# A graph-attention layer: the last 64 edges in one column, the last sums loaded early, the closing projections reordered behind 16 unused products, and the few rows handled later

## The chip, the cores and the metric

The kernel runs on one core of a Trainium2 chip. The core has five engines with a queue each: PE (TensorE, matrix products), DVE (VectorE), ACT (ScalarE), POOL (GpSimd) and SP (SyncE, here only for issuing DMAs). The metric is the device time of one execution in microseconds (us), as the median of repeated runs. Less is better.

## The reference

N = 12500 nodes, E = 212500 edges sorted by destination, 128 features, 8 heads of 16, float32. Cut to what matters:

```python
h = relu(layernorm(x))
q, k, v = h @ Wq.T + bq, edge_attr @ Wk.T + bk, h @ Wv.T + bv
qs, qd = q[src], q[dst]
in_m, out_m, diag_m = sum(qs * k), sum(qd * k), sum(qs * qd)     # per head
score = (softmax(in_m / 4) + softmax(out_m / 4) + softmax(diag_m / 4)) * edge_weight
                                  # softmax over the edges of one destination
h = segment_sum(score * v[dst], dst)
out = x + leaky_relu(h @ Wo.T + bo, 0.1)
```

Since v[dst] is the same for all edges of a destination, a node's h is v times a sum over its edges of exp terms with and without the edge's weight; only these sums (2 x 24 numbers a node) are gathered over edges.

## The kernel before, in words

The edges are cut into 415 groups of 512 (four columns of 128), in five segments of 83 blocks; group g is block t = g // 5 of segment s = g % 5. The last 84 edges don't fill a group. Of these, 64 form a block 83 (called G in the code) that is done after the loop, and the last 20 are the "few rows", done apart.

For each group the loop does: `turn` (PE transposes the 512 edge rows, L1273, and ACT copies them, L1275), `project` (PE: k, L1281 and its bias L1282), `spread_q` (PE: a one-hot times a window of q's rows gives qd, L1289, copied by ACT, L1292), `logits` (DVE: three products, L1300 to L1302, and a reduction, L1303). The rows q[src] come by an indirect DMA that GpSimd issues (L719), four to a group, 26 groups ahead (`LOOK`), into a ring of 28 tiles; the gather for group g + 26 waits on purpose for the projection of group g. SP loads windows (L690), edges (L699), edge bounds (`heads` L742, `tops` L745) and sources (L642). In groups 0 to 4 ACT also issues five DMAs that blank the DRAM tables `sums[s]` (L1778). Every five groups, a block's segment maxima are scanned (DVE), exponentials taken (ACT, L1413), and the sums over each destination's edges made as products with one-hot selections (PE, L1459, and L1470 for the last three blocks) and written to `sums[s]` (`put_rows`, L1480).

The order of every engine's queue is fixed by the order in which the code is written (`pin`). So an instruction that waits holds back all that stand behind it on its engine.

The few rows: `gather_few` (L757 to L763) loads their 20 edge rows and gathers 40 rows of q by one indirect DMA on POOL (L760), which stands behind 116 other gathers; `part_few` (L766) copies 20 of these rows within the chip by a DMA on SP, in group 1; `logits_few` (L1338 to L1358) makes their logits in group 6, in small steps on PE, ACT and DVE.

The nodes: most (two units of 256 nodes at a time) are finished inside the loop. For the rest, the end after the loop does: blocks G-2 = 81, G-1 = 82 and G = 83 (`powers`, `weigh_powers`, `show_ends`, `to_rows`, `put_rows`), then the two pairs of units called `leaving` and `last_pair`, then five groups of the object list `rest` (r0 to r4; r4 is half a group). A group's steps are: `load_last` (L1182: the sums, of two segments for some nodes: `ends_ab` and `more`), a join of the two (L1823), `halves_of` (L1146), `scores_of` (DVE, L1150 to L1153), `weigh` (L1224: v times score), `turn` (PE transposes, L1203, ACT copy to hT, L1206), `project_o` (PE: bias L1209 and product L1211; ACT: scaled copy, L1235), `add_x` (maximum L1241, addition of x L1242) and `store` (L1248, L1250). Before the change, SP loads `ends_ab` and ACT loads `more`, both after the puts; DVE joins r0 and GpSimd r1 to r4; each group is turned and projected before the next one is turned.

Of the kernel before, what the change touches and what calls it, by code (L numbers as in the profile page):

```python
# [16 lines left out]
HEADS = 8  # L17
# [455 lines left out]
def ordered_path(ctx: ExitStack, tc: tile.TileContext, flag, x, src, dst, edge_attr, edge_weight,  # L473
# [184 lines left out]
    def fetch(t):  # L658
# [16 lines left out]
        to = [mybir.EngineType.SP] if t < G else [mybir.EngineType.SP, mybir.EngineType.Activation]  # L675
# [3 lines left out]
        if t == G:  # L679
            for inst in loads:  # L680
                pin(inst)
# [473 lines left out]
    class Nodes:  # L1155
# [51 lines left out]

        def product(self, to, bias, w):
            pin(nc.tensor.matmul(to[:, :self.n, :], ones3, bias[:, :self.n, :], start=True, stop=False))  # L1209
            for b in range(self.n):  # L1210
                pin(nc.tensor.matmul(to[:, b, :], self.hT[:, b, :], w, start=False,  # L1211
                                     stop=(b == self.n - 1)))
# [17 lines left out]
        def project_o(self, to):  # L1230
            n = self.n
            self.product(to, bo3, wo)
            o = self.h[:, :n]
            self.held = to
            pin(nc.scalar.activation(o, to[:, :n], AF.Copy, scale=SLOPE))  # L1235
# [8 lines left out]
        def store(self):  # L1244
            for i, u in enumerate(self.of):
                y = self.x[:, 2 * i:2 * i + 2, :].rearrange("p k f -> p (k f)")
                if u < NU - 1:
                    pin(nc.sync.dma_start(units(out, u, 1, F)[:, 0, :], y))  # L1248
                else:
                    pin(nc.sync.dma_start(out[u * UN:, :].rearrange("(p k) f -> p (k f)", k=2),  # L1250
                                          y[:LAST, :]))
# [13 lines left out]
    with tc.tile_pool(name="work", bufs=2) as work, \  # L1265
# [19 lines left out]
        def spread_q(g):  # L1285
# [7 lines left out]
            del ohs[g]  # L1293
# [16 lines left out]
        for i in range(2):  # L1310
            ends_t.append(scan.tile([K4, P], BF, name=f"ends_t{i + 2}", bufs=1))
            nc.vector.memset(ends_t[-1][0:1, :], 1.0)

# [73 lines left out]
        def scan_back(t):  # L1387
# [5 lines left out]
            else:  # L1393
                head = st[t - 1]["head"]
                m = d["m"] = scan.tile([R, HEAD], F32, name="m_end", bufs=1)
                pin(nc.vector.tensor_sub(m, head, l_end))

        def turn_max(t):
            d = st[t]
            n, width = (P, BE) if t < G else (HEAD // JN, HEAD)  # L1400
            m_ps = d["mT"] = small([P, JN, R], "m_ps")
            for j in range(JN):
                pin(nc.tensor.transpose(m_ps[:n, j, :], d["m"][:, j:width:JN], ident[:R, :R]))  # L1403

        def powers(t):
            d = st[t]
            mT = d["mT"].rearrange("p j (s c) -> p j s c", s=S)
            if t < G:
                back = work.tile([P, JN, S, 2, H3], F32, name="back")
# [4 lines left out]
                d["weigh"] = [(back, 0, JN)]  # L1414
                del lTs[t]
            else:
                n = HEAD // JN
                d["back"], d["weigh"] = [], []
                for j in range(0, JN, 2):
                    half = fin.tile([P, JN, F], F32, name="x_in", bufs=5).rearrange("p j f -> p (j f)")  # L1420
                    half = half[:, :2 * S * 2 * H3].rearrange("p (j s i c) -> p j s i c", j=2, s=S, i=2)
                    pin(nc.scalar.activation(half[:n, :, :, 0, :], mT[:n, j:j + 2], AF.Exp, scale=-SCALE))
                    d["back"] += [half[:, 0], half[:, 1]]
                    d["weigh"].append((half, j, j + 2))

        def weigh_powers(t):
            at, part = block_rows(t)
            n = P if t < G else HEAD // JN
            for back, lo, hi in st[t]["weigh"]:
                att = att_t[:, part, lo:hi].rearrange("p (s b) j -> p j s b", b=G)[:, :, :, at:at + 1]  # L1430
                pin(nc.vector.tensor_mul(back[:n, :, :, 1, :], back[:n, :, :, 0, :],  # L1431
                                         att[:n].to_broadcast([n, hi - lo, S, H3])))

        def select(t):
            at, part = block_rows(t)
            ends = ends_t[t % 2 if t < G - 1 else t - G + 3]
            pin(nc.sync.dma_start(ends[1:, :], rel_d[part].rearrange("(s b) (j p) -> s b j p", b=G, j=JN)
                                  [:, at, :, :]))

        def show_ends(t):  # L1440

            sel = st[t]["sel"] = work.tile([P, JN, S, W], F32, name="sel", bufs=3)
            for i in range(0, JN, 2):
                d = small([P, 2, S, W], "d_ps")
                pin(nc.tensor.matmul(d.rearrange("p j s w -> p (j s w)"), ends_t[t % 2 if t < G - 1 else t - G + 3],
# [5 lines left out]
        def to_rows(t):  # L1451
            d = st[t]
            n = P if t < G else HEAD // JN
# [14 lines left out]
            for s in range(S):  # L1468
                for j in range(JN):
                    pin(nc.tensor.matmul(w_ps[:, s, :], d["sel"][:n, j, s, :],  # L1470
                                         d["back"][j][:n, s].rearrange("p i c -> p (i c)"),
                                         start=(s == 0 and j == 0), stop=(s == S - 1 and j == JN - 1)))
            pin(nc.scalar.copy(rows[:W, :S], w_ps))
# [61 lines left out]
        def begin_rest(at):  # L1535
# [14 lines left out]
            if at == DRAIN - 1:  # L1550
                for of in rest:
                    of.more = None
                    if any(len(parts_of(u)) > 1 for u in of.of):
# [3 lines left out]
                        pin(nc.gpsimd.memset(of.more, 0.0))  # L1557
# [91 lines left out]
        def show():  # L1649
            pin(nc.vector.tensor_copy(shows, show_end.rearrange("k (s j) -> k j s", j=JN)[:, :, :, None]  # L1650
                                      .to_broadcast([K4, JN, S, W])))
            pin(nc.vector.tensor_copy(shows[0:1], show_row[:, None, None, :].to_broadcast([1, JN, S, W])))

# [47 lines left out]
        for g in range(end):  # L1701
# [67 lines left out]
            if 0 < g <= S + 1:  # L1769
                load_bounds(g - 1)  # L1770
            if g == 7:
# [16 lines left out]
        turn_max(G - 2)  # L1788
        scan_on(G)
# [12 lines left out]
        weigh_powers(G - 1)  # L1802
        to_rows(G - 1)
        put_rows(G - 1)
# [79 lines left out]
```

## Time and profile before

| | us |
|---|---|
| median of 3 runs (lowest, highest) | 2182.34 (2178.96, 2182.61) |
| the profiled execution | 2183.8 |
| its span | 2182.0 |
| busy: PE, DVE, ACT, POOL | 1705.6, 1991.4, 1384.9, 1594.6 |
| end of the loop's last reduction (L1303) | 2123.6 |
| last store issued (L1250) | 2175.5 |
| mean granted PE clock | 0.831 |

How to read what follows: a group row of the page has line, engine, operation, tiles, count, then busy us and the mean ns of one, then the idle time before it and what ended it. A row of the waits has who waited, for whom, then us in total, times, and the longest. A row of a timeline has the start, the length, the engine, the line and the operation; in brackets the engine's idle time before it and what ended it. `x8` means that so many instructions stand in that row, and "issue" that nothing the profile shows was waited for. ACTq, SPq and POOLq are the engines' DMA issues. A row of the windows has the stretch, its length, the busy time and count of PE, PEld (weight loads), DVE, ACT and POOL, the granted PE clock, the DMA engines' mean busy share and GB/s.

### The profile page before, as it was taken

Reading aid. Unit: us, or ns where it says so; the run is one execution under the profiler, and the core shown is the slowest. Engines: PE = TensorE matmul, PEld = TensorE weight load, DVE = VectorE, ACT = ScalarE, POOL = GpSimd, SP = SyncE. Lnnn points to the kernel's source line nnn. Section 1 sums busy time; section 2 is a strip of 40 time slices with the busy share of each in tenths; the row PEclk is TensorE's granted clock in tenths of the full one; section 3 lists DMA queues with packets and bytes.
Section 4 is the critical chain, followed back from the end, with each engine's and each line's share of the span. In section 5 each row is a group of like instructions: output and inputs, shape, how many; then the busy total and the mean of one; then the engine's idle time right before and its main releaser. Section 6 shows DMA issues by size and latency. Waiting matters only on the chain.

```text
span 2182.0 us, 36286 instructions
## 1 busy us (share of the span) xinstructions
PE 1705.6 (78%) x10956; PEld 1327.6 (61%) x10956; DVE 1991.4 (91%) x2785; ACT 1384.9 (63%) x2743; POOL 1594.6 (73%) x1683
## 2 busy tenths in 40 slices
PE   5757878887878888888888888877777777678885
PEld 3546756665666666666666666655565565556664
DVE  6758899999999999999999999999898899898995
ACT  5656866666666666666666666665555665566672
POOL 7775677777777777777777777777777777777761
PEclk8877888898888988888878888887888898888786
DMA  9756466666667667665665755566555655556632
GB/s 258 216 159 187 136 174 169 174 166 183 167 173 180 176 170 190 171 168 155 168 172 147 184 158 163 147 163 158 159 143 146 160 156 163 148 154 164 164 92 65
DMA packets 370345, 356.97 MB, mean 164 GB/s; under 512 B 189022, under 2 KB 285097, under 8 KB 369933
## 3 DMA queue, kind: packets, MB, share of 16 engines
q1 hardware_dynamic: 301403, 239.37, 40.1%
q0 software_dynamic: 53152, 108.92, 19.8%
q10 hardware_dynamic: 15584, 6.27, 1.1%
q8 instruction: 89, 1.46, 0.3%
q14 instruction: 117, 0.96, 0.1%
HBM read 322.10 MB, written 32.22 MB: 162 GB/s over the span
## 4 chain that ended last, share of the span: by engine, by line
DVE 42%; DMA 20%; issue 12%; PE 12%; POOL 7%; ACT 5%; SPq 2%; DVEq 0%; ACTq 0%; POOLq 0%
DMA qq<-q_table,sources 16%; DVE lT L1303 11%; POOL qq L719 7%; DVE prod L1300 6%; DVE prod L1301 6%; DVE prod L1302 6%; PE k_ps L1281 3%; DVE l_ps L1363 3%; DVE m L1391 2%; DVE back L1412 2%; PE eT_ps L1273 1%; PE w_ps L1459 1%; DMA ea<-in_edge_attr_dram 1%; DVE back L1431 1%; PE node_ps L1211 1%
## 5 line engine op out<-in xcount | busy, mean ns | idle before, releaser
L719 POOL DMA_INDIRECT qq<-q_table,sources x1564 | 1487.0, 951 | 501.8 <-issue 328.6
L1303 DVE TENSOR_REDUCE lT<-prod 128x96 f32<-128x1536 f32 x415 | 727.4, 1753 | 14.3
L1281 PE MATMUL k_ps<-wk,eT 128*128 128x128 f32 x3320 | 563.5, 324 | 95.3 <-DVE prod L1302 89.9
L1281 PEld LDWEIGHTS k_ps<-wk,eT 128*128 128x128 f32 x3320 | 502.8, 232 | 139.6 <-DVE prod L1302 133.5
L1273 PE MATMUL eT_ps<-ident,ea 128*128 128x128 f32 x1660 | 305.6, 314 | 199.7 <-ACT eT L1275 129.3
L1273 PEld LDWEIGHTS eT_ps<-ident,ea 128*128 128x128 f32 x1660 | 223.2, 162 | 244.8 <-ACT eT L1275 160.9
L1300 DVE TENSOR_TENSOR prod<-qq,k_ps 128x512 f32<-128x512 f32 x412 | 279.1, 678 | 65.4 <-DMA qq<-q_table,sources 51.5
L1301 DVE TENSOR_TENSOR prod<-qq,qd_ps 128x512 f32<-128x512 f32 x412 | 279.9, 679 | 30.7 <-ACT qd L1292 30.6
L710 ACT ACTIVATE relb<-relb,before 126x512 bf16<-126x512 bf16 x415 | 302.4, 729 | 0.0
L1275 ACT COPY eT<-eT_ps 128x512 f32<-128x512 f32 x415 | 241.6, 582 | 66.9 <-PE eT_ps L1273 39.5
L1302 DVE TENSOR_TENSOR prod<-qd,k_ps 128x512 f32<-128x512 f32 x415 | 281.7, 679 | 0.0
L1292 ACT COPY qd<-qd_ps 128x512 f32<-128x512 f32 x415 | 236.8, 570 | 66.1 <-PE qd_ps L1289 65.7
L711 ACT ACTIVATE oh<-relb 126x512 bf16<-126x512 bf16 x415 | 261.4, 630 | 13.2
L1413 ACT ACTIVATE back<-back 128x480 f32<-128x480 f32 x83 | 50.1, 603 | 287.4 <-DVE back L1412 284.0
L1459 PE MATMUL w_ps<-back,sel 128*126 128x144 f32 (+1 forms) x1296 | 169.0, 288 | 41.9 <-ACT sel L1449 40.3
L1459 PEld LDWEIGHTS w_ps<-back,sel 128*126 128x126 f32 (+1 forms) x1296 | 156.7, 186 | 50.2 <-ACT sel L1449 48.6
L1289 PE MATMUL qd_ps<-win,oh 126*128 126x128 bf16 x1660 | 182.7, 239 | 0.0
L1282 PE MATMUL k_ps<-b,ones 3*128 3x512 bf16 x415 | 181.3, 437 | 0.0
L1289 PEld LDWEIGHTS <-oh 126*128 126x128 bf16 x1660 | 103.9, 104 | 115.0 <-issue 115.0
L1366 ACT COPY carry<-l_ps 120x1 f32<-120x1 f32 x81 | 12.9, 159 | 226.5 <-DVE l_ps L1363 221.1
L1403 PE MATMUL m_ps<-ident,m 120*128 120x120 f32 x332 | 75.5, 366 | 42.3 <-DVE m L1391 41.9
L1391 DVE TENSOR_TENSOR_SCAN m<-far,head,l_ps 120x512 f32<-120x512 bf16 x81 | 102.9, 1271 | 0.0
(237 smaller groups left out, 1835.4 us busy)
## 6 DMA issues: line engine op xcount, KB each, us to landing
ea<-in_edge_attr_dram SPq DMA_DIRECT2D x83, 768.0 KB
relb<-rel_d SPq DMA_DIRECT2D x83, 630.0 KB
ea<-in_edge_attr_dram SPq DMA_DIRECT2D x83, 512.0 KB
qq<-q_table,sources POOLq DMA_INDIRECT x1564
win<-q_table SPq DMA_DIRECT2D x415, 31.5 KB
far<-far_d SPq DMA_DIRECT2D x42, 270.0 KB
q_table<-q SPq DMA_DIRECT2D x24, 384.0 KB
sums<-rows SPq DMA_DIRECT2D x411, 7.9 KB
```

Of the source, the lines that this page charges most:

```text
L710: pin(nc.scalar.activation(d, d, AF.Abs, bias=before[:K3]))
L711: pin(nc.scalar.activation(oh, d, AF.Relu, bias=1.0, scale=-1.0))
L719: rows = pin(nc.gpsimd.indirect_dma_start(out=qq[:, j, :], out_offset=None, in_=x if g < RAW else q_table, in_offset=bass.IndirectOffsetOn ...
L1273: pin(nc.tensor.transpose(eT_ps[:, j, :], eas[g][:, j * F:(j + 1) * F], ident))
L1275: pin(nc.scalar.copy(eT, eT_ps))
L1281: pin(nc.tensor.matmul(k_ps[:, j, :], eTs[g][:, j, :], wk, start=(j == 0), stop=False))
L1289: pin(nc.tensor.matmul(qd_ps[:, j, :], ohs[g][:, j * P:(j + 1) * P], d["win"][:, s, :], start=(j == 0), stop=(j == JN - 1)))
L1300: pin(nc.vector.tensor_mul(prod[:, :, 0, :], qqs[g], ks[g]))
L1301: pin(nc.vector.tensor_mul(prod[:, :, 1, :], qqs[g], q_ps[g]))
L1302: pin(nc.vector.tensor_mul(prod[:, :, 2, :], qds[g], ks[g]))
L1303: pin(nc.vector.tensor_reduce(lTs[t][:, :, s, :], prod.rearrange("p j i (h d) -> p j (i h) d", d=DIM), AX.X, ALU.add))
L1459: pin(nc.tensor.matmul(w_ps[:(hi - lo) * W, lo:hi].rearrange("p s c -> p (s c)"), d["sel"][:n, j, lo:hi, :].rearrange("p s w -> p (s w)"), ...
```

## The change

1. **The few rows later.** `part_few` is issued in group 16 (block 3) instead of group 1, `logits_few` in group 21 (block 4) instead of group 6. The gather on POOL stays where it is.
2. **The last 64 edges in one column.** Block G used four columns of 16 edges; now it has 64 partitions and one column: 1 transposition for 4, 5 products for 20, one exponential and one weighing for two. Its weights are loaded by four small DMAs (`load_att`) in groups 54, 59, 64 and 69, its selection uses a table `shows_g` made in group 7.
3. **The order of the end.** Block G's steps now come before those of block G-1; the row copy of G-1 is on DVE; two of its five puts go to ACT's queue; `leaving` is projected after the last pair's turn.
4. **The sums.** The second parts (`more`) are loaded in group 409 by SP, and no longer cleared by GpSimd; their halves are added early; the first parts are loaded by SP. DVE joins r0 and r1, GpSimd r2 to r4, and only the columns that have two parts.
5. **Turnings a group ahead.** The five biases of `rest` are issued early (`begin_product`), each group is turned before the product of the group ahead of it, and 16 products into a PSUM tile that nothing reads (`unused`) stand between the biases and r0's turn.
6. **Stores.** The four of `leaving` and `last_pair` and the very last one are issued by ACT.

```diff
-                if t == 0:
+                if t == 3:
                     part_few(rows_few)
-                elif t == 1:
+                elif t == 4:
                     logits_few()
...
+            if s == 4 and 10 <= t < 10 + JN:
+                load_att(t - 10)
...
+        def begin_product(self, to, bias):
+            pin(nc.tensor.matmul(to[:, :self.n, :], ones3, bias[:, :self.n, :], start=True, stop=False))
...
-            if at == DRAIN - 1:
+            if at == 6:
...
-                        pin(nc.gpsimd.memset(of.more, 0.0))
+                        of.load_last(of.more, nc.sync, 1)
...
         scan_back(G - 1)
         powers(G - 2)
+        scan_back(G)
         turn_max(G - 1)
-        scan_back(G)
-        show_ends(G)
         turn_max(G)
-        leaving.project_o(small([P, JN, F], "node_ps"))
+        weigh_powers(G - 2)
+        to_rows(G - 2)
+        powers(G)
         powers(G - 1)
-        weigh_powers(G - 2)
-        powers(G)
-        to_rows(G - 2)
         put_rows(G - 2)
-        weigh_powers(G - 1)
-        to_rows(G - 1)
-        put_rows(G - 1)
         weigh_powers(G)
-        leaving.add_x(nc.vector)
-        leaving.store()
         to_rows(G)
         put_rows(G, q=nc.scalar)
-        for which, q in ((0, nc.sync), (1, nc.scalar)):
-            for r, of in enumerate(rest):
-                of.load_last(ends_ab[:, r * JN:r * JN + of.n] if which == 0 else of.more, q, which)
+        weigh_powers(G - 1)
+        to_rows(G - 1, nc.vector.tensor_copy)
+        put_rows(G - 1, range(3))
+        put_rows(G - 1, range(3, S), nc.scalar)
+        for of in rest:
+            if of.more is not None:
+                halves_of(of.more[:, of.both], nc.gpsimd)
         last_pair.scores()
         last_pair.weigh(last_pair.held)
         last_pair.turn(small([P, JN, P], "node_ps"))
+        leaving.project_o(small([P, JN, F], "node_ps"))
         last_pair.project_o(small([P, JN, F], "node_ps"))
+        leaving.add_x(nc.vector)
+        leaving.store(nc.scalar)
         last_pair.add_x(nc.vector)
-        last_pair.store()
+        last_pair.store(nc.scalar)
...
+        for r, of in enumerate(rest):
+            of.load_last(ends_ab[:, r * JN:r * JN + of.n], nc.sync, 0)
+            of.begin_product(places_o[r], bo3)
+        unused = small([P, JN, F], "unused")
+        for _ in range(16):
+            pin(nc.tensor.matmul(unused.rearrange("p j f -> p (j f)"), minus_b[:K3, :], now["oh"],
+                                 start=True, stop=True))
...
+        for r in range(2, len(rest)):
+            join(r, nc.gpsimd)
+        begin_end(0)
+        for r in range(1, len(rest) - 1):
+            begin_end(r)
+            rest[r - 1].project_o(places_o[r - 1], begun=True)
+            if r > 1:
+                leave(r - 2)
+        rest[-2].project_o(places_o[-2], begun=True)
+        begin_end(len(rest) - 1)
+        leave(len(rest) - 3)
+        rest[-1].project_o(places_o[-1], begun=True)
+        leave(len(rest) - 2)
+        leave(len(rest) - 1, nc.scalar)
```

`begin_end(r)` is the join (for r0 and r1), the scores, the weighing and the turn of group r; `leave(r)` is its `add_x` (GpSimd's addition for r0 to r2, DVE's for r3 and r4) and its store.

**Where it moves instructions.** SP's queue about group 1, before. `qq<-qq` is the copy of part_few, `win` a window of q's rows, `heads` and `tops` the edge bounds:

```order
L642 DMA sources<-in_src_dram 128x5x4
L766 DMA qq<-qq 20x128
L690 ISA
L690 DMA win<-q_table 126x128
L742 DMA heads<-in_dst_dram 1x84x1
L745 DMA tops<-in_dst_dram 1x84x1
L666 DMA relb<-rel_d 126x5x512
```

And the same place after the change:

```order
L642 DMA sources<-in_src_dram 128x5x4
L690 ISA
L690 DMA win<-q_table 126x128
L742 DMA heads<-in_dst_dram 1x84x1
L745 DMA tops<-in_dst_dram 1x84x1
L666 DMA relb<-rel_d 126x5x512
```

The copy no longer stands between the sources and the window; the same rows follow each other without it, and it comes three loads of sources later.

PE's queue after the loop, before. `node_ps<-ident,h` is the turn of the last pair, `node_ps<-ident,qq` that of a group of `rest`, `ones` with `b` a bias, and `wo` a projection:

```order
L1211 MATMUL node_ps<-wo,hT 128x128 x4
L1470 MATMUL w_ps<-back,sel 42x48 x40
L1470 MATMUL w_ps<-x_in,sel 42x48 x20
L1203 MATMUL node_ps<-ident,h 128x128 x4
L1209 LDWEIGHTS ones_90
L1209 MATMUL node_ps<-b_96,ones_90 128x512
L1211 MATMUL node_ps<-wo,hT 128x128 x4
L1203 MATMUL node_ps<-ident,qq 128x128 x4
L1209 LDWEIGHTS ones_90
L1209 MATMUL eT_ps<-b_96,ones_90 128x512
L1211 MATMUL eT_ps<-wo,qq 128x128 x4
L1203 MATMUL node_ps<-ident,qq 128x128 x4
```

After, the row products of blocks G-2, G and G-1 and the projections behind them:

```order
L1495 MATMUL w_ps<-back,sel 42x48 x20
L1495 MATMUL w_ps<-x_in,sel 42x48 x5
L1495 MATMUL w_ps<-back,sel 42x48 x20
L1203 MATMUL node_ps<-ident,h 128x128 x4
L1209 LDWEIGHTS ones_90
L1209 MATMUL node_ps<-b_96,ones_90 128x512
L1215 MATMUL node_ps<-wo,hT 128x128 x4
```

The products of the 64 edges stand between those of the two whole blocks and are 5 in place of 20, and `leaving`'s projection, which stood ahead of them all, has come behind the last pair's turn. Behind the last pair's projection stand the five biases, 16 products like the first row below, and then:

```order
L1859 MATMUL unused<-oh,minus_b 128x512
L1203 MATMUL node_ps<-ident,qq 128x128 x8
L1215 MATMUL eT_ps<-wo,qq 128x128 x4
L1203 MATMUL node_ps<-ident,qq 128x128 x4
L1215 MATMUL k_ps<-wo,qq 128x128 x4
L1203 MATMUL node_ps<-ident,qq 128x128 x4
L1215 MATMUL qd_ps<-wo,qq 128x128 x4
L1215 MATMUL k_ps<-wo,qq 128x128 x4
```

Two turns stand ahead of the first projection, and each later turn but the last one stands a group ahead of its projection.

More of the change, by code (lines that the diff above doesn't have):

```diff
@@ L1292, in spread_q @@
             pin(nc.scalar.copy(qds[g], qd_ps))
-            del ohs[g]
+            now["oh"] = ohs.pop(g)
         def logits(g):
@@ L1426, in weigh_powers @@
-        def weigh_powers(t):
-            at, part = block_rows(t)
[L1428 to L1432, printed above, removed]
+                back = fin.tile([P, JN, F], F32, name="x_in", bufs=5).rearrange("p j f -> p (j f)")
```

133 lines of the change are left out of this document (82 added, 51 removed).

## The prediction

> **What bounds the kernel now.** I read the page first (its spans, groups and slices), then GpSimd's waits and its gathers after 272 us, then the waits of the first 165 us, then the end after the loop. The profiled execution took 2183.8 us, a span of 2182.0 and 1.8 around it, 1.5 above the median of the three runs (2182.34); sums are made against the span, and the last step goes back to the median.
>
> From the page, the costliest group; then GpSimd's gathers from 272 us on, and its waits between 120 and 330 us:
>
> ```profile
> L719 POOL DMA_INDIRECT qq<-q_table,sources x1564 | 1487.0, 951 | 501.8 <-issue 328.6
> L719 POOL DMA_INDIRECT qq<-q_table,sources x1468: 940/945/1421, 272.4 to 2115.5; - x184
> POOL qq L719 <- issue: 32.3, 106, 0.3
> POOL qq L719 <- PE k_ps L1282: 26.3, 12, 6.4
> POOL qq L719 <- DMA tops<-in_dst_dram: 2.1, 1, 2.1
> ```
>
> From 272.4 to 2115.5 us GpSimd issues 1468 gathers, one every (2115.5 - 272.4) / 1467 = 1.256 us: 0.945 of work and the 0.30 that every gather has before it as "issue". That is a stream without a hole, over 85% of the span. VectorE is busier (91% on the page), but it needs the gathered rows, so the stream sets when the loop ends. Whatever lets it stand earlier at 272 us lets the loop end earlier by as much. Before that it has holes: 13 waits of 28.4 us together, less 13 x 0.30 of ordinary issue, 24.5 us. Twelve of them are for the projection of the group 26 before (L1282), whose place in the ring the gather takes. So that stage is paced by the groups, not by GpSimd. Why the groups are late stands in SyncE's and the other waits of the first stage:
>
> ```profile
> SPq L766 <- DMA qq<-q_table,few_i: 16.4, 1, 16.4
> PE eT_ps L1273 <- ACT eT L1275: 19.5, 1, 19.5
> ACT eT L1275 <- DMA tops<-in_dst_dram: 19.2, 1, 19.2
> 138.16 1.65 ACT L733 ACTIVATE qq<-qq,raw_shift,raw_inv 128x128 f32<-128x128 f32 x4
> 158.60 0.38 ACTq L1778 DMA_DIRECT2D sums<-jp  x1
> 154.07 0.85 SPq L766 DMA_DIRECT2D qq<-qq  x1
> 155.14 0.37 SPq L690 DMA_DIRECT2D win<-q_table  x1
> 156.43 0.76 SPq L745 DMA_DIRECT2D tops<-in_dst_dram  x1
> 151.77 0.92 POOL L760 DMA_INDIRECT qq<-q_table,few_i  x1 [0.30 <-issue]
> ```
>
> SyncE stands 16.4 us at the copy of part_few (L766), which it issues at 154.07. That copy needs the gather of the few rows, which stands in GpSimd's queue at 151.77. Behind the copy on SyncE stand the window load, heads and tops (156.43). ScalarE's third blanking store (L1778) needs the tops load; ScalarE is done with its work at 138.16 + 1.65 = 139.81 and issues at 158.60. TensorE, whose transposes wait for a copy behind that store, stands for 19.5 us.
>
> **The change part by part.** *Few rows later.* part_few moves from group 1 to group 16, logits_few from group 6 to group 21. The few gather stays at 151.77, so the copy at group 16 finds it landed and waits for nothing. SyncE's next instruction, the window load, now waits only for what else L766 waited for: the 16.4 us row is the part of its wait that came last, so SyncE goes on at 154.07 - 16.4 = 137.67. The copy's own slot goes as well (155.14 - 154.07 = 1.07). Tops is issued at 156.43 - 17.47 = 138.96, and the blanking store at 158.60 - 17.47 = 141.13, 1.3 after ScalarE is free. So the groups behind it start 17.5 us earlier, if nothing else is late next. What may be late next is the DMA:
>
> ```profile
> 100.00:140.00 40.00, 32.28 (x225) 25.75 (x224) 27.38 (x58) 32.23 (x73) 30.24 (x33) 0.91 0.80 226
> 140.00:160.00 20.00, 0.53 (x3) 0.34 (x4) 3.06 (x7) 0.97 (x2) 15.12 (x17) 0.63 0.30 69
> 160.00:180.00 20.00, 15.27 (x74) 13.26 (x72) 12.39 (x21) 11.77 (x27) 9.64 (x11) 0.60 0.98 264
> 180.00:200.00 20.00, 16.30 (x109) 13.36 (x108) 17.04 (x33) 15.02 (x35) 11.03 (x12) 0.83 0.65 176
> 182.72 0.56 PE L1346 MATMUL few_ps<-wk,few_eT 128*20 128x128 f32 x2 [1.59 <-ACT few_eT L1343]
> 184.63 0.20 PE L1355 MATMUL few_ps<-ident,few_l 20*24 20x20 f32 x1 [1.34 <-DVE few_l L1352]
> ```
>
> The last two columns are the DMA's busy share and GB/s. From 100 to 200 us it is busy 0.80 x 40 + 0.30 x 20 + 0.98 x 20 + 0.65 x 20 = 70.6 of 100 us. Squeezed into 82.5 us that is 0.86. It fits, but the stretch that stands at 0.98 now will be longer. The bounds: no cost, and at worst the stage paced at what the DMA does now at 0.98; I take 2 us of the 17.5, an estimate, and keep 0 to 8. Moving the logits of the few rows takes their waits on TensorE (1.59 + 1.34, about 3 us with VectorE's part) out of group 6 and puts them behind projection 22, where the same 3 us come back before projection 23, still inside the paced stage: nothing net. The four small loads of the weights of the 64 edges go to SyncE in groups 54 to 69 and two small copies to VectorE in group 7; in the stream's shadow they cost nothing, and without it half a us each. Gain of the stage: 15.5 us, from 10 to 17.5; the 24.5 us of holes are the ceiling, since a hole-free stream can't start earlier.
>
> *The end.* Rows of VectorE, ScalarE, TensorE, SyncE after the loop:
>
> ```profile
> 2139.74 0.69 DVE L1224 TENSOR_TENSOR h<-h,score 128x512 f32<-128x512 f32 x1
> 2150.28 0.70 DVE L1241 TENSOR_TENSOR node_ps<-h,node_ps 128x512 f32<-128x512 f32 x1 [9.84 <-ACT h L1235]
> 2151.62 1.25 DVE L1823 TENSOR_TENSOR ends_ab<-ends_ab,qq 128x384 f32<-128x384 f32 x1
> 2153.57 0.88 DVE L1150 TENSOR_SCALAR ends_ab<-ends_ab 128x96 f32<-128x96 f32 x1
> 2155.86 0.69 DVE L1224 TENSOR_TENSOR qq<-qq,end_score 128x512 f32<-128x512 f32 x1
> 2158.08 0.69 DVE L1224 TENSOR_TENSOR qq<-qq,end_score 128x512 f32<-128x512 f32 x1
> 2173.99 0.43 DVE L1241 TENSOR_TENSOR qd_ps<-qq,qd_ps 128x256 f32<-128x256 f32 x1 [0.54 <-ACT qq L1235]
> 2140.94 3.21 ACTq L1480 DMA_DIRECT2D sums<-rows  x5
> 2144.42 2.44 ACTq L1182 DMA_DIRECT2D qq<-sums  x4
> 2146.90 0.59 ACT L1206 COPY hT<-node_ps 128x512 f32<-128x512 f32 x1 [6.53 <-DMA sums<-rows]
> 2156.70 1.09 PE L1203 MATMUL node_ps<-ident,qq 128*128 128x128 f32 x4 [7.08 <-DVE ends_ab L1150]
> 2161.33 0.60 PE L1209 MATMUL k_ps<-b,ones 3*128 3x512 bf16 x1
> 2162.07 2.08 PE L1211 MATMUL k_ps<-wo,qq 128*128 128x128 f32 x8
> 2165.68 2.08 PE L1211 MATMUL qd_ps<-wo,qq 128*128 128x128 f32 x8
> 2160.00:2170.00 10.00, 9.58 (x37) 7.07 (x37) 7.33 (x15) 3.56 (x6) 3.34 (x3) 0.50 0.15 52
> 2172.31 1.22 PE L1211 MATMUL qd_ps<-wo,qq 128*128 128x128 f32 x4 [0.20 <-ACT qq L1206]
> 2175.47 0.29 SPq L1250 DMA_DIRECT2D out_dram<-qq  x1
> L1289 PE MATMUL qd_ps<-win,oh 126*128 126x128 bf16 x1660 | 182.7, 239 | 0.0
> 137.88 0.40 PE L1289 MATMUL qd_ps<-win,oh 126*128 126x128 bf16 x4
> ```
>
> ScalarE copies the last pair's hT at 2146.90 only because nine DMA issues stand ahead of it, and what follows hangs on that copy. The change sends the loads of `more` out in the loop's last groups, beside work that hides them (that cover gone, they cost their 2.44 again), and the other five from SyncE; the 64 edges in one column need 5 products for 20, one exponential and one weighing for two. ScalarE keeps seven puts. The row copy before them now stands ahead of block 82's products and not behind them, which is 3 to 5 us earlier than 2140.94, an estimate; seven puts at 3.21 / 5 are 4.5 us, so hT is free to be copied by about 2142. The last pair's scores end where they end now (2139.74 + 0.69 = 2140.4) or half a us later, since a row copy comes to VectorE ahead of them and an add_x goes from there. Then TensorE: turn 0.9, `leaving` 0.6 + 2.1, last pair 0.4 + 2.1, to 2147.3. ScalarE's 0.6 and VectorE's two of 0.7 bring both pairs to 2149.3; now 2151.7. For r0 VectorE then halves and joins, about 1.0 us in place of a join of 1.25 and a halving (the halves of `more` are done early), and scores, 2158.08 - 2155.86 = 2.2 a group where GpSimd doesn't join beside it. r0 is weighed at about 2152.5; now 2155.86 + 0.69 = 2156.55. That is 4 us.
>
> TensorE, though, has 5 biases and the 16 unused products to do before r0's turn. No row shows such a product. From above it is bounded by the bias of the same 128 x 512: 0.60 at granted clock 0.50, so 21 of them 12.6 us, to 2159.9. That row holds a latency that overlaps within a run, as the last two rows show: four products of 128 columns take 0.40 where one takes 0.24, a step of (0.40 - 0.24) / 3 = 0.053. Four steps make 512 columns, 0.21 at a clock of 0.91 (the row of 100 to 140 us), 0.39 at 0.50. So 21 take 8.2 us, to 2155.5, if the clock stays, 4.4 us if it were 0.91 from the start. I take the middle, 2153.6, one us behind r0: this run is 8 us without a break.
>
> From there the order puts the next group's turn ahead of each product, and the copy that TensorE waits for now is hidden. A group then takes TensorE 0.9 + 2.1 = 3.0 at clock 0.50, where it takes 2165.68 - 2162.07 = 3.6 now. VectorE has, after r0: 2.2 for each of r1 to r3, 1.6 for the half r4, a join of 1.0, maxima and two adds of together 4.3: 13.5 us, so 2166, and about 2167 with TensorE's us; TensorE still at 0.50 would make it 2155.5 + 13.6 (five turns of 0.9 and products of 2.08, the last group's 0.6 and 1.22) + 1.3 (from 2172.31 + 1.22 to VectorE's end) = 2170.4. VectorE's end now is 2173.99 + 2 x 0.43 = 2174.9, so 8 or 4.5 us. The tail from the last store (2175.47) to 2182.0, 6.5 us, I leave, though ScalarE issues that store now. I take 6, from 2 to 9.
>
> The clock: the end has 0.50 in a stretch where TensorE is busy 9.58 of 10 us, so being busy alone doesn't raise it here; the 8 us of products without a break may. [...]
>
> Sum: 15.5 + 6 = 21.5 us. 2182.3 - 21.5 = 2160.8, rounded 2161.
>
> **The rivals.** *The loop gives it back.* The saved 17.5 us come back as late loads, the 0.98 stretch being as long as now: ten of the 15.5 lost, 2161 + 10 = 2171. For it speaks the 0.98, against it 0.86 over the stage. Chance 0.12.
>
> *Every hole goes.* If the shift frees the ring for good, all 24.5 go: 2182.3 - 24.5 - 6 = 2152. Against it: the shift moves the paced groups by 17.5 and makes none of them shorter, and 24.5 is more. 0.05.
>
> *The unused products hold the end.* Cold to the end at 0.60 each, r0's turn is at 2159.9, 3 later than now (2156.70), and with the same 13.6 and 1.3 us the end is 2174.8: no gain there. 2182.3 - 15.5 = 2167. 0.11.
>
> *Slower: ScalarE's seven puts.* Each of them waits for an earlier block's store to the same sums, and the copy of hT stands behind all. If they and SyncE's eight landed strictly one after another, at the 2.5 us that one took:
>
> ```profile
> 2143.82 2.55 DMA sums<-rows
> ```
>
> then 15 x 2.55 = 38 us from about 2137, hT at 2175 and not 2142, 33 us more: 2161 + 33 = 2194. It decides from 26 us of delay on, that is when more than a dozen landings stand in a row. Against it: five puts now take ScalarE 3.21 us. 0.03.
>
> **How the numbers follow.** Forecast 0.69, rivals 0.12, 0.05, 0.11 and 0.03. Its own range is 12 to 26 us of gain, 2156 to 2170. The range 2154 to 2171 takes that, the third rival, half of the first and a little of the second, and leaves 2 in 10 out. 0.2% is 4.4 us, about what a measurement can tell here. All but the fourth rival are faster by more, save the first with the third together: faster 0.93, same 0.04, slower 0.03.
>
> **What would show it.** Right: SyncE's wait at L766 gone, ScalarE's 19.2 us wait at most 3, the last gather at about 2100; in the end hT by 2142 counted from the same loop end, r0 weighed 4 us earlier, TensorE's clock above 0.50 behind the unused products. Wrong: last gather within 5 us of 2115 (the loop gave it back), r0's turn waiting for TensorE by more than 3 us, or a ScalarE wait for a put of over 10.

## The result, and the profile after

The changed kernel takes 2159.05 us, the median of 8 runs, beside 2177.73 for the kernel before in as many runs by then: a ratio of 0.9912, 95% interval 0.9891 to 0.9933. That is 19.2 us less (14.6 to 23.7). The forecast was 21.5 us less and 2161. The kernel before came out 4.6 us lower than in the three runs that the prediction had (2182.34), and its profiled execution, at 2183.8, lies above all eight; so differences of the two profiled executions overstate the change.

The profile after: the page's span and costliest group, GpSimd's gathers from 250 us on, then the waits that answer to those of before (SyncE's, ScalarE's, TensorE's in the first stage, GpSimd's from 120 to 330 us).

```profile
span 2157.1 us, 36250 instructions
L719 POOL DMA_INDIRECT qq<-q_table,sources x1564 | 1485.2, 950 | 481.1 <-issue 317.9
L719 POOL DMA_INDIRECT qq<-q_table,sources x1467: 940/944/1419, 249.6 to 2092.9; - x184
SPq L690 <- DMA sums<-jp: 8.9, 1, 8.9
PE eT_ps L1277 <- ACT eT L1279: 8.6, 2, 4.4
ACT eT L1279 <- DMA ea<-in_edge_attr_dram: 5.1, 1, 5.1
ACT eT L1279 <- DMA tops<-in_dst_dram: 3.9, 1, 3.9
POOL qq L719 <- PE k_ps L1286: 5.5, 7, 3.1
POOL qq L719 <- PE few_ps L1365: 1.3, 1, 1.3
142.39 0.38 ACTq L1809 DMA_DIRECT2D sums<-jp  x1
```

The 16.4 us row of SyncE is gone; what is left is the part of its wait that stood ahead of it (8.9, before 9.1). ScalarE's third blanking store goes out at 142.39 where it went out at 158.60. TensorE's 19.5 us have become 8.6. GpSimd's waits for the projections fell from 26.3 us to 5.5, and the last gather starts at 2092.9 and not 2115.5. Its busy time is the same (1485.2 and 1487.0), its idle time isn't. The loop's last reduction ends 8.4 us behind the start of the last gather (2101.26 and 2092.9), and before it was 8.1 behind (2123.6 and 2115.5), so the loop ends earlier by about as much as the gathers do. So the gain of the loop is where the prediction put it. One wait is new: the fourth blanking store, held 5.1 us by an edge load.

The end, from VectorE, TensorE, ScalarE and GpSimd:

```profile
2099.51 1.75 DVE L1307 TENSOR_REDUCE lT<-prod 128x96 f32<-128x1536 f32 x1
2117.57 0.40 DVE L1498 COPY rows<-w_ps 42x240 f32<-42x240 f32 x1 [2.05 <-DMA sums<-rows]
2119.89 0.69 DVE L1228 TENSOR_TENSOR h<-h,score 128x512 f32<-128x512 f32 x1
2131.30 0.69 DVE L1228 TENSOR_TENSOR qq<-qq,end_score 128x512 f32<-128x512 f32 x1
2147.76 0.42 DVE L1246 TENSOR_TENSOR qq<-qd_ps,qq 128x256 f32<-128x256 f32 x1
2120.64 1.12 PE L1203 MATMUL node_ps<-ident,h 128*128 128x128 f32 x4 [3.10 <-DVE h L1228]
2128.79 6.25 PE L1859 MATMUL unused<-oh,minus_b 126*128 126x512 bf16 x16
2134.88 1.04 PE L1203 MATMUL node_ps<-ident,qq 128*128 128x128 f32 x8
2136.16 1.16 PE L1215 MATMUL eT_ps<-wo,qq 128*128 128x128 f32 x8 [0.24 <-ACT qq L1206]
2113.81 0.35 ACT L1498 COPY rows<-w_ps 42x240 f32<-42x240 f32 x1 [4.27 <-PE w_ps L1495]
2115.79 3.78 ACTq L1505 DMA_DIRECT2D sums<-rows  x7
2121.79 0.59 ACT L1206 COPY hT<-node_ps 128x512 f32<-128x512 f32 x1 [6.02 <-PE node_ps L1203]
2145.52 1.27 POOL L1246 TENSOR_TENSOR qq<-qq 128x512 f32<-128x512 f32 x1 [2.43 <-DVE qq L1245]
2121.00:2127.00 6.00, 6.00 (x23) 4.23 (x22) 1.39 (x2) 1.31 (x3) 2.65 (x5) 0.50 0.46 140
2127.00:2130.00 3.00, 3.00 (x8) 0.87 (x7) 2.30 (x6) 0.47 (x1) 0.00 (x0) 0.50 0.31 109
2130.00:2133.00 3.00, 3.00 (x8) 1.06 (x7) 2.72 (x8) 0.00 (x0) 0.00 (x0) 0.50 0.19 66
```

I count from the end of the loop's last reduction, 2099.51 + 1.75 = 2101.26 here and 2123.6 before. To the span's end it is 55.8 us here, 58.4 before: 2.6 less. r0 is weighed at 2131.30 + 0.69 = 2131.99, 30.7 behind; before 32.9. But its turn starts at 2134.88, 33.6 behind, where it started 33.1 behind before: TensorE was still at the unused products, 2.9 us too long. The last three rows show why they took so long: TensorE had no break from 2121 to 2133 and stayed at a granted clock of 0.50 throughout. Behind the unused products a projection takes 1.16 in place of 2.08; the granted clock is 1.00 from 2136 to 2140 us.

### The profile page after: what moved, and what is told of

It is laid out like the page before. It is cut to its first block, busy times and chain, and to the rows that moved or that the text cites. A ratio compares the mean times of both kernels' runs of the same rounds, so it can differ in the third digit from the quotient of the medians.

```text
span 2157.1 us, 36250 instructions
## 1 busy us (share of the span) xinstructions
PE 1701.3 (79%) x10938; PEld 1320.0 (61%) x10938; DVE 1991.5 (92%) x2789; ACT 1382.5 (64%) x2740; POOL 1590.6 (74%) x1681
## 4 chain that ended last, share of the span: by engine, by line
DVE 39%; DMA 20%; issue 13%; PE 13%; POOL 6%; ACT 6%; SPq 2%; DVEq 1%; ACTq 0%; POOLq 0%
DMA qq<-q_table,sources 15%; DVE lT L1307 10%; POOL qq L719 6%; DVE prod L1304 6%; DVE prod L1305 6%; DVE prod L1306 6%; PE k_ps L1285 3%; DVE l_ps L1373 3%; DVE m L1401 3%; PE w_ps L1484 2%; DVE back L1427 2%; DMA sums<-rows 2%; PE eT_ps L1277 1%; PE node_ps L1215 1%; PE k_ps L1286 1%
## 5 line engine op out<-in xcount | busy, mean ns | idle before, releaser
L719 POOL DMA_INDIRECT qq<-q_table,sources x1564 | 1485.2, 950 | 481.1 <-issue 317.9
```

Of the source, the lines that this page charges most:

```text
L719: rows = pin(nc.gpsimd.indirect_dma_start(out=qq[:, j, :], out_offset=None, in_=x if g < RAW else q_table, in_offset=bass.IndirectOffsetOn ...
```

## The experiments

Theory A: SyncE's wait at part_few makes nearly all of the gain, the reordered end a few us, and the 16 products pay about what they cost. Rivals: half of the gain comes from the end (B), the logits of the few rows also held the first stage (C), the unused products only hold the end (D), the clock that they may bring is worth more than they cost (F), GpSimd's closing sets the end (G).

The runs came in three series (the recorded expectations say "call"), each on a chip of its own and with the kernel before beside it. "From the reduction" is the time from the end of the loop's last reduction to the end of the span, in the one profiled execution.

| run | series: kernel before, us | ratio (95%) | from the reduction, us |
|---|---|---|---|
| e0, the changed kernel | 1: 2178.89 | 0.9909 (0.9894 to 0.9923) | 51.8 |
| e1, few rows later alone | 1 | 0.9916 (0.9901 to 0.9932) | 58.4 |
| e2, all but that | 1 | 0.9985 (0.9976 to 0.9994) | 55.9 |
| e5, the copy alone later | 1 | 0.9920 (0.9904 to 0.9936) | 60.2 |
| e3, no unused products | 2: 2660.03 | 0.9986 (0.9975 to 0.9998) | 57.4 |
| e8, 32 of them | 2 | 0.9986 (0.9973 to 0.9999) | 57.9 |
| e4, 16 of them earlier | 2 | 0.9971 (0.9960 to 0.9982) | 51.1 |
| e6, r2's addition on VectorE | 2 | 0.9974 (0.9963 to 0.9986) | 55.1 |
| e12, the changed kernel | 3: 2180.12 | 0.9914 (0.9900 to 0.9928) | 54.0 |
| e9, no unused products | 3 | 0.9907 (0.9892 to 0.9922) | 55.7 |
| e10, 16 of them earlier | 3 | 0.9907 (0.9892 to 0.9922) | 55.3 |
| e11, 16 earlier, 8 late, r2 on VectorE | 3 | 0.9892 (0.9876 to 0.9909) | 52.1 |

**e0, the changed kernel again.** No edit.

> The changed kernel once more, beside e1, e2 and e5 on one chip, so that the parts can be added up. Measured so far: 0.9912 of the kernel before, 19 us less. Both theories expect 15 to 22 us less; a run outside of that would say that the parts can't be compared by medians at all.

19.8 us less (16.8 to 23.1), as expected. In its profiled execution TensorE was faster, and the same 16 products were done before r0 was weighed (TensorE's rows):

```profile
2124.66 3.63 PE L1859 MATMUL unused<-oh,minus_b 126*128 126x512 bf16 x16
2128.97 0.63 PE L1203 MATMUL node_ps<-ident,qq 128*128 128x128 f32 x4 [0.68 <-DVE qq L1228]
```

3.63 us for 16, not 6.25 (in e4, too, they took 3.63, at a granted clock of 1.00), and TensorE waits for VectorE and not the other way. The end took 51.8 us, 4.0 less than the execution above, with the same instructions.

**e1, the few rows later, alone** (in the kernel before):

```diff
-                if t == 0:
+                if t == 3:
                     part_few(rows_few)
-                elif t == 1:
+                elif t == 4:
                     logits_few()
```

> The kernel before with part_few in group 16 and logits_few in group 21, nothing else. Theory A (the saved wait of SyncE at part_few carries nearly all of the change): SyncE's 16.4 us wait is gone, ScalarE's 19.2 us wait falls to under 5, GpSimd's last gather starts 17 to 23 us before 2115.5, and the time falls by 16 to 20 us, 80% or more of the changed kernel's gain in this call. Rival B (half of the gain comes from the reordered end): 8 to 12 us.

18.3 us less (14.8 to 21.6): 92% of e0's 19.8. Its gathers, and GpSimd's waits for a projection:

```profile
L719 POOL DMA_INDIRECT qq<-q_table,sources x1475: 940/944/1432, 239.5 to 2092.7; - x185
POOL qq L719 <- PE k_ps L1282: 2.9, 6, 0.7
```

The last gather starts 22.8 us ahead of 2115.5, more than the time gained; the execution that has 2115.5 lies above its kernel's median (e2 has a better pair). SyncE's wait for the few rows is gone, and ScalarE's for tops is 4.2 us. B's 8 to 12 us lie outside the interval.

**e2, all but that** (the changed kernel with groups 1 and 6 again; the reverse of e1's diff).

> The changed kernel with part_few and logits_few put back into groups 1 and 6, so the end, the 64 edges in one column and the early loads alone. Theory A: the traces give 58.4 us from the loop's last reduction to the end of the span before and 55.8 after, so the time falls by 2 to 3 us, inside what can be told. Rival B: 6 us or more, as was predicted for the end.

3.3 us less (1.3 to 5.2). B's 6 us lie outside the interval. SyncE's wait at the copy is back, with GpSimd's:

```profile
SPq L766 <- DMA qq<-q_table,few_i: 17.5, 1, 17.5
POOL qq L719 <- PE k_ps L1286: 21.1, 10, 5.3
```

e2 and e0 differ in the place of the few rows alone. Their gathers, e2's first:

```profile
L719 POOL DMA_INDIRECT qq<-q_table,sources x1488: 940/944/1433, 239.8 to 2109.0; - x186
L719 POOL DMA_INDIRECT qq<-q_table,sources x1475: 940/944/1432, 239.3 to 2092.5; - x185
```

The last one starts 16.5 us earlier in e0.

e1 and e2 add up to 21.6 against e0's 19.8, inside the intervals.

**e5, only the copy later** (in the kernel before):

```diff
+                if t == 1:
+                    part_few(rows_few)
                 later(turn_head, t - 1)
...
-                if t == 0:
-                    part_few(rows_few)
-                elif t == 1:
+                if t == 1:
                     logits_few()
```

> The kernel before with only the copy of part_few moved, from group 1 to the end of group 5, just ahead of logits_few in group 6, which stays. Theory A (it is the copy's wait, the logits moved nothing for good): the gathers shift by 17.5 us in the end, and the time falls by 15 to 18 us. Rival C (the logits of the few rows in group 6 also hold the paced stage): a shift smaller by 3 to 4 us than in e1, and TensorE's and VectorE's waits for the few rows (1.6, 1.3 and 2.6 us) are back in group 6.

17.4 us less (13.9 to 20.9), not to be told from e1. The intervals alone don't exclude rival C's 3 to 4 us, but the gathers speak against them: the last one starts at 2091.7 here and at 2092.7 in e1, so the shift isn't smaller. That is one execution of each. SyncE still waits a little at the copy, and the logits' wait is in group 6; GpSimd loses 5.3 us to projections, in other groups than the changed kernel, which loses 5.5:

```profile
SPq L766 <- DMA qq<-q_table,few_i: 2.2, 1, 2.2
PE few_ps L1355 <- DVE few_l L1352: 1.4, 1, 1.4
POOL qq L719 <- PE k_ps L1282: 5.3, 7, 2.8
```

**e3, no unused products.**

```diff
-        for _ in range(16):
-            pin(nc.tensor.matmul(unused.rearrange("p j f -> p (j f)"), minus_b[:K3, :], now["oh"],
-                                 start=True, stop=True))
```

> The changed kernel without its 16 unused products; all else as changed. Theory A (they pay about what they cost: they hold r0's turn by up to 2.9 us, and give the clock back to the products behind them): r0's turn starts within 0.3 us of r0's weighing, TensorE then takes 2.08 for a product and 0.9 for a turn at clock 0.50, the span from the loop's last reduction to the end is 54 to 57 us, and the time is within 3 us of the changed kernel's. Rival D (they only hold the end): 3 us or more faster than the changed kernel, a ratio of 0.989 or less. Rival F (the clock they bring is worth more): 3 us or more slower, 0.9925 or more.

This series ran on a chip where the kernel before takes 2660 us. Two rows of e3 show a loop with another bound: GpSimd's group with its idle time, then TensorE's wait for nothing that the profile shows.

```profile
L719 POOL DMA_INDIRECT qq<-q_table,sources x1564 | 1483.3, 948 | 849.9 <-issue 354.4
PE eT_ps L1277 <- issue: 190.1, 90, 6.8
```

A gather takes what it took (948 ns), but GpSimd is idle 850 us and not 481; TensorE stands up to 6.8 us at a time. Its last gather starts at 2476.8, which is 123.0 us ahead of the end of the loop's last reduction; in the other series it is 8 to 10 us in every trace. So GpSimd runs far ahead of its users here and its stream is no bound, and all four kernels of this series, which hold the few rows' part of the change, gain 0.1 to 0.3% instead of 0.9. So the 18 us seem to belong to a loop that GpSimd's stream bounds; e1 wasn't run there. What made the engines stand on that chip isn't known. The ends after the loop look as in the other series, so these traces are used for the end.

Without the unused products: 0.9986, with the turns right behind the weighings; the changed kernel itself was not in this series, so e9 and e12 compare the two in another.

**e8, 32 unused products** (`range(32)`).

> The changed kernel with 32 unused products in place of 16, all in the same place. Theory A: the further 16 take 16 x 0.21 = 3.5 us at a full clock to 16 x 0.39 = 6.3 at 0.50, all ahead of r0's turn, which is already late or just in time; so r0's turn starts 3 to 6 us behind r0's weighing and the end is 2 to 5 us later than in the changed kernel. Rival F: the clock is full for the rest of the end in every run, and the time is the same or less.

0.9986 as e3, so by time not told apart. TensorE's rows:

```profile
2631.56 8.48 PE L1859 MATMUL unused<-oh,minus_b 126*128 126x512 bf16 x32
2639.87 1.04 PE L1203 MATMUL node_ps<-ident,qq 128*128 128x128 f32 x8
2641.15 1.16 PE L1215 MATMUL eT_ps<-wo,qq 128*128 128x128 f32 x8 [0.24 <-ACT qq L1206]
```

r0's two turns stand together behind them: r0 and r1 had both been weighed while TensorE was at them, and r0's turn started 5.1 us behind its weighing. The end took 57.9 us, 0.5 more than e3's. What they cost and what they bring can't be told apart here.

**e4, the 16 products earlier**, ahead of the last pair's turn:

```diff
         last_pair.weigh(last_pair.held)
+        unused = small([P, JN, F], "unused")
+        for _ in range(16):
+            pin(nc.tensor.matmul(unused.rearrange("p j f -> p (j f)"), minus_b[:K3, :], now["oh"],
+                                 start=True, stop=True))
         last_pair.turn(small([P, JN, P], "node_ps"))
```

(and taken out behind the biases).

> The changed kernel with the 16 unused products moved from behind the last pair's projection to ahead of the last pair's turn, where TensorE waits 3.1 us for VectorE's scores. Theory A: at a full clock they take 3.5 us there and cost 0.4, nothing holds r0's turn, and the two projections and five biases behind run at a full clock more often: 1 to 3 us faster than the changed kernel. Rival F (they have to stand right ahead of r0's turn to help): the clock is down again when r0's turn comes, TensorE takes 3.0 us a group, and the time is the same or more.

0.9971, the best of its series, and an end of 51.1 us. In its trace everything is as theory A has it:

```profile
2611.40 1.87 PE L1495 MATMUL w_ps<-back,sel 128*42 128x48 f32 x40 [0.29 <-DVE back L1446]
2613.20 3.63 PE L1846 MATMUL unused<-oh,minus_b 126*128 126x512 bf16 x16
2625.39 1.09 PE L1203 MATMUL node_ps<-ident,qq 128*128 128x128 f32 x4 [4.23 <-DVE qq L1228]
```

At a granted clock of 1.00 (2610 to 2620 us) the 16 take 3.63 us in a time in which TensorE would wait for VectorE, and r0's turn waits for r0 (4.23), not for TensorE.

**e6, r2's addition of x on VectorE.**

```diff
-            rest[r].add_x(nc.gpsimd if r < len(rest) - 2 else nc.vector)
+            rest[r].add_x(nc.gpsimd if r < 2 else nc.vector)
```

> The changed kernel with the addition of x for r2 on VectorE in place of GpSimd. In the changed kernel's trace GpSimd's last addition ends 45.5 us behind the loop's last reduction and its closing steps (semaphores, 1.6 us of one instruction, a drain of 5.8) end 9.5 us later, after SyncE's; the last additions being VectorE's, GpSimd is done 3 us earlier. Theory A: the tail is then set by the landing of the last store, and the time falls by 0 to 1.5 us, inside what can be told; the trace shows GpSimd's closing drain ending ahead of SyncE's waits. Rival G (GpSimd's drain sets the end alone): 2.5 to 3 us faster.

0.9974 in the second series, which has no changed kernel beside it, so the time says nothing. The trace has GpSimd's and VectorE's last additions and the span:

```profile
2640.41 1.27 POOL L1246 TENSOR_TENSOR qq<-qq 128x512 f32<-128x512 f32 x1 [1.82 <-DVE qq L1245]
2646.45 0.42 DVE L1246 TENSOR_TENSOR qq<-qd_ps,qq 128x256 f32<-128x256 f32 x1
span 2655.1 us, 36250 instructions
```

GpSimd is done 13.4 us before the end (10.3 in the changed kernel), yet from VectorE's last addition to the end it is 8.2 us, where the changed kernel has 8.9. GpSimd's closing drain, its last long instruction (5.8 us in the changed kernel), ends 2.8 us ahead of the end of SyncE's own closing waits here; in the changed kernel it ends 0.3 us behind it, and in the kernel before 0.8 ahead of it. So rival G's 2.5 to 3 us are out.

**e12 and e9, the changed kernel and none of the unused products, in one series.**

> The changed kernel once more, as the reference of this call: the call with e3, e4, e6 and e8 had a kernel before of 2660 us, and the changed kernel wasn't in it. Both theories: 0.988 to 0.993 if the kernel before is at about 2180 us; if it is at 2660 again, where the engines stand for reasons the profile doesn't show and GpSimd's stream isn't the bound, theory A expects the loop's part to shrink with it, 0.996 to 0.999.

> The changed kernel without the 16 unused products, as e3. Theory A: within 3 us of the changed kernel in this call, TensorE's turns right behind VectorE's weighings, 55 to 58 us from the loop's last reduction to the end. Rival D (the unused products only hold the end): 3 us or more faster. Rival F (their clock is worth more): 3 us or more slower.

0.9914 and 0.9907: not told apart, and D's and F's 3 us (0.0014) aren't excluded by either interval alone, though neither shows in the medians (2160.01 and 2161.77). In e12's trace r0's turn starts 3.2 us behind its weighing, as the unused products took 6.5 us, which is at the edge of what the prediction named as a sign of being wrong (more than 3); in e9's it follows at once. How far one execution can lead astray is seen in the gathers of the two, e9's first:

```profile
L719 POOL DMA_INDIRECT qq<-q_table,sources x1476: 938/944/1434, 241.1 to 2099.2; - x185
L719 POOL DMA_INDIRECT qq<-q_table,sources x1475: 940/944/1426, 240.2 to 2091.3; - x185
```

The code is the same up to the end, and the last gather is 7.9 us apart.

**e10, e4 once more.**

> The 16 unused products ahead of the last pair's turn, as e4, whose end took 51.1 us from the loop's last reduction. Theory A: 50 to 53 us again and no wait of r0's turn for TensorE, so 2 to 4 us faster than the changed kernel and than the one without unused products. Rival F (a chance of the clock's windows in e4): no faster than the changed kernel, an end of 54 us or more.

Here theory A missed: 0.9907, no better than e9, and an end of 55.3 us where e4 had 51.1. TensorE's rows again:

```profile
2120.23 3.43 PE L1495 MATMUL w_ps<-back,sel 128*42 128x48 f32 x40
2123.59 3.77 PE L1846 MATMUL unused<-oh,minus_b 126*128 126x512 bf16 x16
2135.96 1.09 PE L1203 MATMUL node_ps<-ident,qq 128*128 128x128 f32 x4 [4.27 <-DVE qq L1228]
```

The 16 are as fast as in e4. But the row products just before them took 3.43 us for e4's 1.87, the granted clock being 0.55 from 2115 to 2125 us where e4 has 1.00 from 2610 to 2620, and the chain was 4 us late before it came to the 16 products, which stayed to the end. So e4's 51.1 owes something to a lucky clock, as theory A's rival had it. Whether the early place is worth anything stays open: the median is 4.1 us under that of no unused products in the second series (e4, e3) and 1.7 under it in the third (e10, e9), and the intervals overlap both times. What is right in theory A is that the products hold nothing at that place.

**e11, 16 earlier, 8 late, and r2's addition on VectorE** (the edits of e4 and e6, and 8 more such products behind the five biases).

> As e10, and 8 more unused products behind the five biases, where TensorE waited 4.2 us for r0 in e4, and r2's addition of x on VectorE. Theory A: 8 x 0.21 = 1.7 us at a full clock fit into that wait; the clock stays up behind r0, so that the products take 1.2 and not 1.9, and the end takes 49 to 51 us: 1 to 2 us less than e10. Rival F: the clock falls all the same, and the time is that of e10.

0.9892 (0.9876 to 0.9909), 23.5 us less than before, the best of all. The changed kernel in the same series has 0.9914; the intervals overlap, so it beats the kernel before and can't be told from the changed one. TensorE's rows show the 8 in the gap:

```profile
2126.60 1.90 PE L1862 MATMUL unused<-oh,minus_b 126*128 126x512 bf16 x8
2131.16 0.63 PE L1203 MATMUL node_ps<-ident,qq 128*128 128x128 f32 x4 [2.66 <-DVE qq L1228]
```

The end took 52.1 us, not the 49 to 51 that was expected.

## Why the prediction was right

**What bounds the loop: right.** That GpSimd's stream without a hole carries a shift of the first stage unchanged to the end is shown by e1: nothing else is changed, and the gain is 18.3 us. That it is GpSimd's stream, and not VectorE with its 92%, is what the gathers say: in all ten traces outside of the second series the loop's last reduction ends 8 to 10 us behind the last gather, early or late; in the second series, where something else bounds the same loop, it is 121 to 123 us.

**The term of the few rows: right.** It was 17.5 us less 2 for the DMA, 15.5; e1 measured 18.3 (14.8 to 21.6), and the gathers of e2 and e0 lie 16.5 apart. Whether the 2 us were needed can't be told from these. The DMA's share did rise where the engines stood before, as these rows of the windows have it:

```profile
140.00:160.00 20.00, 12.19 (x62) 10.22 (x63) 12.42 (x26) 11.09 (x23) 15.12 (x17) 0.69 0.97 247
160.00:180.00 20.00, 15.76 (x121) 13.14 (x119) 19.59 (x35) 17.41 (x38) 15.12 (x17) 0.97 0.82 233
```

0.97 and 0.82 in place of 0.30 and 0.98. GpSimd went through both at its full rate (15.12 of 20 us, 17 instructions; before 9.64 and 11 in the second). So nothing shows that the DMA held the stage for long. A detail was missed: "ScalarE's 19.2 us wait at most 3" is 3.9 now, and the edge load holds the next blanking store for 5.1.

**The logits of the few rows: right.** "Nothing net" was the working; e1 and e5 differ by 0.0004, and their last gathers by 1.0 us, e5's being the earlier.

**The end: the term mis-sized.** 6 us, from 2 to 9, were taken; e2 measured 3.3 (1.3 to 5.2). By the traces of the first and third series the new end took 54.4 us on average (the changed kernel, e0, e2, e12) and the old one 59.0 (the kernel before, e1, e5), 4.6 less. Which part of the end brings this (the 64 edges in one column, the sums loaded early, the order, the turns ahead) isn't shown, since they ran only together. Three steps of the working failed in the execution of the changed kernel that was profiled first.

"r0 is weighed 4 us earlier" was 2.2, since the row products of block 81 ran at a granted clock of 0.52 (3.40 us; in e0 1.87, which those of block 82 took in this trace at 1.00) and ScalarE waited for them (4.27) ahead of the exponential of block 82. The last pair's scores, which were to end "where they end now" or half a us later, hang on this too: the last row copy now stands ahead of them on VectorE and started at 2117.57, and they ended 19.3 us behind the loop's last reduction, before 16.8. In e0 they ended at 17.2, and r0 was weighed 5.5 us earlier. So the working rested on the clock of one execution. (Its 13.6 us of TensorE's turns and products add up to 13.7, which changes nothing.)

"I take the middle" for the five biases and 16 products, 6.3 us: they took 2126.76 to 2135.0, the 8.2 that the working had for 0.50 (the granted clock of that stretch is 0.55), and began later, so they held r0's turn until 2.9 us behind r0's weighing, where the forecast had 1 and the third rival 7.4 (2159.9 - 2152.5). That a run without a break lifts the clock was the author's estimate, and no run shows it: TensorE had no break from 2121 us on and stayed at 0.50 until 2133. The step of 0.39 us a product at 0.50 was right: 6.25 / 16 = 0.39, and in e4 3.63 / 16 = 0.23 at 1.00 (0.21 at 0.91 by the working).

"The tail I leave" at 6.5 us behind the last store: from VectorE's last addition to the end it is 8.9 us and was 2182.0 - 2174.9 = 7.1, so 1.8 us went back. The old end has 9.4 in e1 and 7.2 in e5, though, and the new one 8.9 to 9.2 in e0, e2 and e12, so how much of this is the change's stays open.

What e0 and e12 add is that no single value of this term is to be had from one execution: the same end took 51.8, 54.0 and 55.8 us.

**The sum: close by luck.** By the medians the loop's part came out above its 15.5 us and the end's below its 6, and the two misses nearly cancel: 18.3 + 3.3 = 21.6 where 21.5 was forecast. The change as a whole measured 19.2.

**The rivals.** *The loop gives it back* is refuted by e1; on the second series' chip, where GpSimd's stream isn't the bound, something like it is what the small gains look like, but no run there was made with the few rows' part alone. *Every hole goes* (24.5) lies outside e1's interval. *The unused products hold the end* is half right: with the 16 behind the biases r0's turn was held by 2.9 to 3.2 us in four traces (the changed kernel, e2, e6, e12) and not in e0. By time this isn't told from having none, and the gain of the end isn't gone. *ScalarE's seven puts* took 3.78 us, and the copy of hT behind them waited for TensorE (6.02) and not for a put.

## What to carry to other kernels

A transfer that waits for something far down another queue must not stand in an in-order queue ahead of loads that the start needs: read what is queued behind the waiting instruction, and who waits for that, and move it behind the point where its input is there anyway; here SyncE stood 16.4 us at the copy, and moving the copy alone saved 17.4. A stall early in a kernel, here at 138 of 2180 us, is worth about its full length if a stream without holes bounds the rest (16.4 us of wait, 18.3 saved in e1); look for that stream first, as the gain need not be there where another bound holds (0.1 to 0.3% in the second series). Where the end depends on TensorE's granted clock, judge it by the median of many runs: here one end took 51.8, 54.0 and 55.8 us. Filling products belong where the engine waits anyway, if anywhere: no run here shows that they gain time.

## What the runs showed of the hardware

- The granted clock of the same stretch of code was 0.50 in one execution and 0.99 in another. e5 and e1 have the same end, and their loops end within 0.2 us; the stretch from 2141 to 2151 us, e5's first:

```profile
2141.00:2151.00 10.00, 9.57 (x37) 7.36 (x36) 5.98 (x13) 2.99 (x6) 3.80 (x3) 0.50 0.18 63
2141.00:2151.00 10.00, 6.21 (x42) 4.65 (x41) 7.80 (x17) 3.57 (x8) 3.80 (x3) 0.99 0.28 94
```

- TensorE stayed at 0.50 through 12 us in which it was busy without a break (2121 to 2133 us of the changed kernel, the rows above). The products bear that record out: the 16 unused ones took 0.39 us each here and 0.23 in e4, at 1.00.
- In e1 the clock went from 0.50 (2131 to 2141 us, TensorE busy 5.00 of 10) to 0.99 (2141 to 2151, busy 6.21 of 10) without any unused product. What raises it isn't shown.
- TensorE's mean granted clock says little of this kernel's time: one of the eight executions of the changed kernel had 0.624 where the others had 0.828 to 0.838, and took 2170.17 us, 11 more than the median. It has no trace, so where the 11 us went isn't known.
